# Group 2's statistics in the prologue, and three elements' attention weights transposed by TensorE, in a two-layer graph kernel

## The chip, the cores and the metric

The kernel runs on one core of a Trainium2 chip. The core has a matrix engine (TensorE, PE in the profile, its weight loads PEld), a vector engine (VectorE, DVE), a scalar engine (ScalarE, ACT), a general engine (GpSimd, POOL) and a queue that issues nearly all DMA transfers here (SyncE, SP). Each executes its own instructions in the order in which they were written; semaphores hold an instruction back until what it needs is there.

The metric is the time of the device for one execution, in microseconds (us). A profile of one execution shows when every instruction started and how long it took.

## The reference

`x` is 128 batch elements of 128 nodes with 512 features, `adj` one weighted 128x128 adjacency matrix with its diagonal. All is fp32.

```python
# layer 0: graph convolution
h = relu(layernorm(x));  norm_adj = adj * d[:, None] * d[None, :]      # d = deg ** -0.5
x = x + einsum('nm,bmo->bno', norm_adj, h @ W0) + b0
# layer 1: attention, 8 heads of 64, masked by adj
h = relu(layernorm(x))
q, k, v = h @ Wq + bq, h @ Wk + bk, h @ Wv + bv
attn = softmax(q k^T / 8 + (1 - adj) * -1e9)
x = x + (attn v) @ Wo + bo
```

## The kernel before

**Tiling.** The 128 elements go through in 32 groups of 4; an element's 128 nodes fill the 128 partitions. A projection (512x512 weights) of a group is computed by a scheme with seven block products instead of eight, in some cases at two levels (`Projection`). It needs sums of blocks of its left side, made by DVE or POOL: `Operands.combine` writes four sums at L362 to L365 and, for the second level, nine more by `combine_one` at L90. Weights get the same at the start: `combine_w` (L264, four sums) and `combine_inner` (L90, nine). The prepared weights are stored to DRAM (`keep_w`, L191) and reloaded for each later group (`reload_w`, L992).

**Rounds.** The main loop runs over rounds t, of blocks W, Q, K, V and Y. Round t computes the graph convolution's projection of group t+1 (W), queries, keys and values of group t (Q, K, V), and the output projection of group t-1 (Y). Each block has seven steps, W0 to W6 and so on. Round 0 has no W and no product in Y. A prologue goes before it: it prepares constants and brings groups 0 and 1 through the first layer, the second with the seven products of `gcn_weight(1)`, between which other work is placed.

**The order of the work.** Nothing reorders at run time. A table `plan` names for each round and place what else is to be issued there: `at(t, "Q3", f, ...)` appends a call to the place Q3 of round t. The function `block` walks through the places, issues the table's calls of step n (place `Q3`), then the product and its first reads (`step(3)`), then the calls of `Q3b`, then further reads (`rest(3)`). One place's calls are in the order of their appending, and those of the prologue are appended last. So each engine's order follows from this walk, SP's too.

**What belongs to one element:** `ln1` and `ln2` compute statistics for half a group: per element one DVE instruction at L314 and one at L315, then `scale`: DVE L319 (`ve`), POOL L320 (`rs`) and two of POOL L322 (`nb`). `gcn_norm` and `norm_h` (ACT L333) apply them and give `h`. `gcn_mix` (PE L605, tile `pa`) multiplies `h` by the adjacency; ACT copies it into the operand tile (L610). `transpose_h` turns `h` of layer 1 by PE (L674, tile `pt`), with a copy by ACT (L675). `gcn_operands` and `attention_operands` call `combine`; in groups 0 and 1 the latter's first four sums run on DVE, in later groups on POOL.

**Attention.** `scores` (PE L750) goes to four PSUM banks; DVE reads it with the mask (L757), or ACT without it (L754) and POOL adds it later (`add_mask`, L765). Then `row_max` (DVE L769), `exponentials` (ACT L777) and `softmax_end` (DVE L784, POOL L785). `attend` needs the weights transposed. In groups 0 to 30 this goes through DRAM: `split_att` has ACT separate the halves of each number (L790) and stores them (`planes`, L791), and `turn_att` reads them back by a DMA transpose on SP (L794), into the buffer of element b-1. In group 31, `transpose_att` does it in place: PE turns eight heads (L801, tile `paT`, through two PSUM buffers that `pa`, `pt`, `pss` and `po` share) and ACT makes two copies (L803). The four calls of `attend` (PE L816, ACT L823) of group t-1 stand at V0 of round t, elements 2 and 3 first; after them come the scores of group t, whose element 1 uses the banks that `attend` of elements 0 and 1 filled.

**Shared buffers around the change.** The tile `op_o` is the operand tile of attention, but before that it holds the weights v (in round 0) and then o (in round 1) while they are prepared: `combine_inner v`, `keep_w v`, `load_w o`, `combine_w o`, `combine_inner o` and `keep_w o` follow each other on it, and then ACT writes the first `attend` result to it.

Of the kernel before, what the change touches and what calls it, by code (L numbers as in the profile page):

```python
# [93 lines left out]
def kernel(  # L94
# [640 lines left out]
    def att_of(g, b):  # L735


        return att_buf[(b - g) % (GB + 1)]

    def scores(g, b):  # L740
        cols = slice(b * P, (b + 1) * P)
        if b == 3:
            pair = [small_bank(f"pss_{g}_{b}_{p}") for p in range(2)]
        else:
            pair = [bank[k] for k in (("b", f"a{1 - turn[0]}") if b == 1 else ("d0", "d1"))]
        pss = [t.rearrange("q (c k) -> q c k", c=NC) for t in pair]
        for c in range(NC):
            for p in range(2):
                rows = slice(p * HD, (p + 1) * HD)
                nc.tensor.matmul(pss[p][:, c, :], qs[g][rows, c, cols], ks[g][rows, c, cols], start=True, stop=True)  # L750
        for p in range(2):
            dst = att_of(g, b)[:, p * NC : (p + 1) * NC, :]
            if masked_apart(g, b):
                nc.scalar.activation(dst, pss[p], AF.Copy, scale=SCALE)  # L754
            else:
                mask = msk.unsqueeze(1).to_broadcast([P, NC, P])
                nc.vector.scalar_tensor_tensor(dst, pss[p], SCALE, mask, ALU.mult, ALU.add)  # L757
# [47 lines left out]
    def attend(g, b):  # L805
        if g not in op_o:
            op_o[g] = op_norm if g == NG - 1 else op_att
        aT = att_of(g, b if g == NG - 1 else b - 1)
        if b == 2 or b == 3:
            po = small_bank(f"po_{g}_{b}")  # L810
        else:
            po = bank["b" if b == 0 else f"a{1 - turn[0]}"]
        for c in range(NC):
            for p in range(2):
                h = 2 * c + p
                nc.tensor.matmul(  # L816
                    po[p * HD : (p + 1) * HD, c * P : (c + 1) * P],
                    vs[g][:, b, h * HD : (h + 1) * HD],
                    aT[:, p * NC + c, :],
                    start=True,  # L820
                    stop=True,
                )
        nc.scalar.copy(op_o[g].blocks_of(b), po.rearrange("p (c n) -> p c n", c=NC))  # L823
# [20 lines left out]
    for t in range(-1, NG + 1):  # L844
# [3 lines left out]
        if 0 <= t - 1 < NG - 1:  # L848
            g = t - 1

            for first, final, place, f, *args in (
                ("W1", "-Y6", "Q0", turn_att, 0),
                ("W4b", "-Y6b", "W1b", split_att, 1),
                ("W5", "-Y3", "W2", exponentials, 2, 0, H // 2),
                ("W6", "-Y4", "W3", exponentials, 2, H // 2, H),
                ("Q0b", "-Y5b", "W4b", softmax_end, 2),
                ("Q1", "-Y5", "W5", exponentials, 3, 0, H // 2),
                ("Q2", "-Y6", "W6", exponentials, 3, H // 2, H),
                ("Q0", "Q1", "Q2", turn_att, 1),
                ("Q2b", "Q0b", "Q0b", softmax_end, 3),  # L860
                ("Q4b", "Q0b", "Q3b", split_att, 2),
                ("Q6b", "Q2", "Q5b", split_att, 3),
                ("K1", "Q2", "K0", turn_att, 2),
                ("K3", "Q5", "K2", turn_att, 3),
            ):
                place = first if t == 1 else final if last else place
                at(t - place.startswith("-"), place.strip("-"), f, g, *args)
            for b in (2, 3, 0, 1):
                at(t, "V0", attend, g, b)
        if t == 0:  # L870

            at(0, "Q0b", ln2, 1, 0)
            at(0, "Q1b", ln2, 1, 1)
            at(0, "K6", norm_h, 1, 0)
            at(0, "K6", norm_h, 1, 1)
            at(1, "W0", transpose_h, 1, 0)
            at(1, "W0", norm_h, 1, 2)
            at(1, "W1", transpose_h, 1, 1)
            at(1, "W1", norm_h, 1, 3)
            at(1, "W2", transpose_h, 1, 2)  # L880
            at(1, "W3", transpose_h, 1, 3)
            at(1, "W3", attention_operands, 1)
            at(2, "W6", attention_residual, 1, 0)
            at(2, "W6", attention_residual, 1, 1)
        elif 1 <= t + 1 < NG and t >= 0:
            g = t + 1
            at(t, "K0b" if g < NG - 1 else "Q0b", ln2, g, 0)
            at(t, "K3b" if g < NG - 1 else "Q3b", ln2, g, 1)
            if g == NG - 1:

                places = ("Q3", "Q4", "Q5", "Q5", "Q6", "Q6", "K1", "K2", "K2")
                steps = ((norm_h, 0), (norm_h, 1), (transpose_h, 0), (norm_h, 2), (transpose_h, 1), (norm_h, 3))
                steps += ((transpose_h, 2), (transpose_h, 3))
            else:
                places = ("V1", "V2", "V2b", "V3", "V5", "V6", "Y1", "Y2", "Y5")
                steps = ((norm_h, 0), (norm_h, 1), (split_h, 0), (split_h, 1), (norm_h, 2), (norm_h, 3))
                steps += ((transpose_h, 2), (transpose_h, 3))
                at(t, "Y0", turn_h, g)
            for place, (f, b) in zip(places, steps):
                at(t, place, f, g, b)  # L900
            at(t, places[8], attention_operands, g)
            at(t + 1, "Q3", attention_residual, g, 0)
            at(t + 1, "Q4", attention_residual, g, 1)
# [5 lines left out]
            at(t, "W5" if t > 1 else "W0", load_x, t + 2, (1,))  # L909
        if 2 <= t + 2 < NG:  # L910
            g = t + 2
            at(t, "Q0b", ln1, g, 0, (0,), ())
            at(t, "Q1b", ln1, g, 0, (1,), (0, 1))
            at(t, "Q3b", ln1, g, 1)
            places = (("Q3", "Q5"), ("Q4", "Q6"), ("Q5b", "K1"), ("Q6", "K2"))
            for b, (norm, mix) in enumerate(places):
                at(t, norm, gcn_norm, g, b)
                at(t, mix, gcn_mix, g, b)
            at(t, "K2" if t > 0 else "V1b", gcn_operands, g)
            at(t, "Y1" if t > 0 else "K3", gcn_residual, g, 0)  # L920
            at(t, "Y2" if t > 0 else "K3", gcn_residual, g, 1)
        if 0 <= t < NG:
# [16 lines left out]
            else:  # L939
# [5 lines left out]
                else:  # L945
# [1 line left out]
                    at(t, "V5b", exponentials, g, 1, 0, H // 2)  # L947
                    at(t, "V6", exponentials, g, 1, H // 2, H)
                    at(t + 1, "W1b", softmax_end, g, 1)
                at(t, "Y3b", split_att, g, 0)  # L950
                at(t, "V6b", row_max, g, 2)
                at(*((t, "Y1") if t > 0 else (1, "W0")), add_mask, g, 3)
                at(*((t, "Y3b" if g == NG - 2 else "Y6b") if t > 0 else (1, "W4b")), row_max, g, 3)
# [67 lines left out]
    def prologue():  # L1021
# [35 lines left out]
        for n, product in enumerate(gcn_weight(1)):  # L1057
# [3 lines left out]
            elif n == 2:  # L1061
                transpose_h(0, 0)
                norm_h(0, 2)
            elif n == 3:
                transpose_h(0, 1)
                norm_h(0, 3)
                combine_w("q", nc.gpsimd)
            elif n == 4:
                transpose_h(0, 2)
            elif n == 5:  # L1070
                transpose_h(0, 3)
                attention_operands(0)
# [91 lines left out]
```

## Time and profile before

| What | us |
|---|---|
| median of 3 runs (lowest, highest) | 2301.77 (2300.41, 2305.13) |
| the profiled execution | 2300.24 |
| its span, first to last instruction | 2298.4 |
| PE busy | 2274.9 (99%) |
| DVE busy | 1863.2 (81%) |
| POOL busy | 1862.8 (81%) |
| ACT busy | 1366.8 (59%) |
| bytes moved by DMA | 566.46 MB, 246 GB/s |

The profiled execution's own time is 1.84 us above its span. Times in a profile count from the start of the span. A row of a timeline gives start, length, engine, line, operation, output and inputs, shapes and count; brackets at the end give the idle time before it and what ended it. Rows merge neighbours of one kind, and matmuls overlap, so a row's length holds the last one's tail. A row of the waits gives the engine, tile and line that waited and what for, the total, how often, and the longest.

### The profile page before, as it was taken

How to read it: one execution, taken by the hardware profiler on the slowest of the kernel's cores; microseconds unless marked ns; L12 is line 12 of the kernel's file. 1: busy time of each engine (PE TensorE's matmuls, PEld its weight loads, DVE VectorE, ACT ScalarE, POOL GpSimd, SP SyncE). 2: the span in 40 equal slices, each digit the busy share in tenths (PEclk: the TensorE clock that was granted, in tenths of full speed). 3: DMA queues.
4: the chain of work that ended last, by engine and by line, in shares of the span. 5: the costliest groups of instructions: out<-in, count | busy, mean ns of one | idle time of the engine just before them, and what ended most of it. 6: DMA issues, size and time to landing. Idle time of an engine off the chain costs nothing.

```text
span 2298.4 us, 50576 instructions
## 1 busy us (share of the span) xinstructions
PE 2274.9 (99%) x18127; PEld 2131.8 (93%) x18127; DVE 1863.2 (81%) x4832; ACT 1366.8 (59%) x3553; POOL 1862.8 (81%) x1927
## 2 busy tenths in 40 slices
PE   8999999999999999999999999999999999999999
PEld 8889999999999999999999999999999999999998
DVE  6778888788888888887888888888877888888876
ACT  3555666655656556566566565566665665655654
POOL 6898888788888787888888887879877788878864
PEclk9999999999999999999999999999999999999999
DMA  6388978889887888788897788987888988789873
GB/s 200 123 260 272 270 247 257 238 251 298 240 253 235 252 269 257 257 244 246 249 304 244 242 240 248 278 258 253 241 248 248 285 251 244 241 249 289 235 230 115
DMA packets 455259, 566.46 MB, mean 246 GB/s; under 512 B 332640, under 2 KB 339936, under 8 KB 454496
## 3 DMA queue, kind: packets, MB, share of 16 engines
q1 hardware_dynamic: 455008, 563.23, 81.2%
q8 instruction: 144, 2.36, 0.4%
q14 instruction: 107, 0.88, 0.1%
HBM read 358.68 MB, written 124.26 MB: 210 GB/s over the span
## 4 chain that ended last, share of the span: by engine, by line
PE 74%; POOL 6%; DMA 6%; DVE 3%; issue 2%; ACT 2%; SPq 0%; POOLq 0%; DVEq 0%; ACTq 0%
PE bank_a L388 27%; PE bank_d L388 16%; PE bank_c L388 8%; PE bank_b L388 8%; PE pa L605 4%; DMA xt<-in_x_dram 4%; PE bank_d L750 3%; PE po L816 3%; POOL xt L337 2%; DVE xt L429 2%; PE pss L750 1%; PE bank_b L816 1%; PE bank_a L816 1%; PE bank_b L750 1%; POOL att L765 1%
## 5 line engine op out<-in xcount | busy, mean ns | idle before, releaser
L777 ACT ACTIVATE att<-att,nmx 128x128 f32<-128x128 f32 x1024 | 396.3, 391 | 0.9 <-DVE nmx L769 0.9
L388 PE MATMUL bank_a<-op_h,w 128*128 128x256 f32 x1488 | 353.3, 380 | 0.0
L785 POOL TENSOR_TENSOR att<-att,rsm 128x1024 f32<-128x1024 f32 x128 | 243.1, 1900 | 80.3 <-DVE rsm L784 79.9
L388 PEld LDWEIGHTS bank_a<-op_h,w 128*128 128x128 f32 x1488 | 270.0, 191 | 29.4
L429 DVE TENSOR_TENSOR xt<-xt,bank_d 128x512 f32<-128x512 f32 x732 | 268.8, 415 | 19.2 <-DVE xt L429 1.4
L790 ACT COPY att<-att 128x2048 uint16<-128x2048 uint16 x124 | 234.9, 1895 | 60.5 <-POOL att L785 60.5
L333 ACT ACTIVATE h<-xt,nb,rs 128x512 f32<-128x512 f32 x254 | 207.3, 817 | 69.2 <-POOL nb L322 67.4
L711 ACT ACTIVATE q<-bank_a,bqk 128x256 f32<-128x256 f32 x192 | 80.6, 471 | 265.4 <-PE bank_a L388 265.4
L320 POOL TENSOR_TENSOR rs<-ve,mhalf 128x2 f32<-128x2 f32 (+1 forms) x129 | 91.3, 708 | 180.1 <-DVE ve L319 179.7
L90 POOL TENSOR_TENSOR op_o<-op_o 128x256 f32<-128x256 f32 x297 | 210.1, 734 | 10.0
L388 PE MATMUL bank_d<-op_h,w 128*128 128x128 f32 (+1 forms) x1712 | 216.9, 278 | 0.7 <-issue 0.3
L90 POOL TENSOR_TENSOR op_a<-op_a 128x256 f32<-128x256 f32 x279 | 197.1, 730 | 14.9 <-DVE op_a L365 5.3
L388 PEld LDWEIGHTS bank_d<-op_h,w 128*128 128x128 f32 x1712 | 203.1, 192 | 5.0 <-issue 3.4
L90 POOL TENSOR_TENSOR op_h<-op_h 128x256 f32<-128x256 f32 x270 | 190.7, 731 | 13.1 <-DVE op_h L365 3.8
L777 ACT ACTIVATION_READ_ACCUMULATOR att<-att,nmx 128x1 f32 x1024 | 194.8, 190 | 0.0
L314 DVE BATCH_NORM_STATS2 st<-xt 128x6 f32<-128x512 f32 x256 | 172.9, 675 | 20.3 <-DMA xt<-in_x_dram 20.0
L388 PE MATMUL bank_a<-w,op_o 128*128 128x256 f32 x768 | 181.7, 379 | 0.0
L388 PE MATMUL bank_a<-w,op_h 128*128 128x256 f32 x744 | 179.1, 384 | 0.0
L388 PE MATMUL bank_a<-w,op_a 128*128 128x256 f32 x744 | 176.9, 381 | 0.2 <-DVE xt L439 0.2
L439 DVE TENSOR_TENSOR xt<-bank_a,xt 128x512 f32<-128x512 f32 x252 | 166.9, 684 | 11.5 <-PE bank_a L388 3.9
L757 DVE SCALAR_TENSOR_TENSOR att<-bank_d,msk 128x512 f32<-128x512 f32 x128 | 82.4, 686 | 104.7 <-PE bank_d L750 96.2
L769 DVE TENSOR_REDUCE nmx<-att 128x8 f32<-128x1024 f32 x128 | 154.9, 1210 | 0.0
(188 smaller groups left out, 5936.2 us busy)
## 6 DMA issues: line engine op xcount, KB each, us to landing
w<-wd_v SPq DMA_DIRECT2D x93, 704.0 KB, 5.6
w<-wd_o SPq DMA_DIRECT2D x93, 704.0 KB, 7.1
planes<-att SPq DMA_DIRECT2D x124, 512.0 KB, 4.5
w<-wd_q SPq DMA_DIRECT2D x90, 704.0 KB, 6.1
w<-wd SPq DMA_DIRECT2D x87, 704.0 KB, 5.6
xt<-in_x_dram SPq DMA_DIRECT2D x63, 512.0 KB, 6.5
out_dram<-xt SPq DMA_DIRECT2D x62, 512.0 KB, 4.1
planes_h<-att SPq DMA_DIRECT2D x29, 512.0 KB, 3.0
```

Of the source, the lines that this page charges most:

```text
L90: engine.tensor_tensor(twice(out), twice(x), twice(y), ALU.subtract if minus else ALU.add)
L314: nc.vector.bn_stats(self.st[:, j, :], self.src[:, j, :])
L333: nc.scalar.activation(h, src[:, j, :], AF.Relu, bias=nb[:, j : j + 1], scale=rs[:, j : j + 1])
L388: nc.tensor.matmul(out, lhsT, rhs, start=start, stop=True, skip_group_check=True)
L429: nc.vector.tensor_tensor(dst, dst, src, f)
L439: nc.vector.tensor_tensor(t, src.rearrange("p (r f) -> p r f", r=2), t, ALU.add)
L750: nc.tensor.matmul(pss[p][:, c, :], qs[g][rows, c, cols], ks[g][rows, c, cols], start=True, stop=True)
L769: nc.vector.tensor_reduce(nmx, att_of(g, b), AX.X, ALU.max, negate=True)
L777: nc.scalar.activation(att[:, h, :], att[:, h, :], AF.Exp, bias=nmx[:, h : h + 1], scale=1.0, accum_out=sm[:, h : h + 1])
L785: nc.gpsimd.tensor_tensor(att, att, rsm.unsqueeze(2).to_broadcast([P, H, P]), ALU.mult)
L790: nc.scalar.copy(planes, halves)
L816: nc.tensor.matmul(po[p * HD : (p + 1) * HD, c * P : (c + 1) * P], vs[g][:, b, h * HD : (h + 1) * HD], aT[:, p * NC + c, :], start=True, s ...
```

## The change

Statistics of group 2 (`ln1(2, 0)` and `ln1(2, 1)`) are issued between the products of `gcn_weight(1)` in the prologue instead of in steps Q0 to Q3 of round 0. Elements 2 and 3 of group 0 and element 3 of group 30 no longer go through `split_att` and `turn_att`; `transpose_att` turns them in place, at K3 and K5 of round 1 and at K1 of round 31, and `attend` reads them where they are. `split_att(0, 0)` moves from Y3b of round 0 to W1 of round 1, `attention_operands(1)` from W3 to W4b of round 1, and the two halves of `attention_residual(1)` from W6 to Q5 and K1 of round 2.

```diff
+    def turned_in_place(g, b):
+        return g == NG - 1 or (g, b) in ((0, 2), (0, 3), (NG - 2, 3))
...
     def attend(g, b):
...
-        aT = att_of(g, b if g == NG - 1 else b - 1)
+        aT = att_of(g, b if turned_in_place(g, b) else b - 1)
...
                 place = first if t == 1 else final if last else place
+                if f in (split_att, turn_att) and turned_in_place(g, args[0]):
+                    continue
                 at(t - place.startswith("-"), place.strip("-"), f, g, *args)
+            if t == 1:
+                at(1, "K3", transpose_att, g, 2)
+                at(1, "K5", transpose_att, g, 3)
+            elif last:
+                at(t, "K1", transpose_att, g, 3)
...
             at(1, "W3", transpose_h, 1, 3)
-            at(1, "W3", attention_operands, 1)
-            at(2, "W6", attention_residual, 1, 0)
-            at(2, "W6", attention_residual, 1, 1)
+            at(1, "W4b", attention_operands, 1)
+            at(2, "Q5", attention_residual, 1, 0)
+            at(2, "K1", attention_residual, 1, 1)
...
-            at(t, "Q0b", ln1, g, 0, (0,), ())
-            at(t, "Q1b", ln1, g, 0, (1,), (0, 1))
-            at(t, "Q3b", ln1, g, 1)
+            if t > 0:
+                at(t, "Q0b", ln1, g, 0, (0,), ())
+                at(t, "Q1b", ln1, g, 0, (1,), (0, 1))
+                at(t, "Q3b", ln1, g, 1)
...
-                at(t, "Y3b", split_att, g, 0)
+                at(*((t, "Y3b") if t > 0 else (1, "W1")), split_att, g, 0)
...
             elif n == 3:
                 transpose_h(0, 1)
                 norm_h(0, 3)
+                ln1(2, 0)
                 combine_w("q", nc.gpsimd)
             elif n == 4:
                 transpose_h(0, 2)
+                ln1(2, 1)
```

## The prediction

> **What bounds the kernel now.** The page first: the span is 2298.4 us and TensorE (PE) is busy for 2274.9 us of it.
>
> ```profile
> span 2298.4 us, 50576 instructions
> PE 2274.9 (99%) x18127; PEld 2131.8 (93%) x18127; DVE 1863.2 (81%) x4832; ACT 1366.8 (59%) x3553; POOL 1862.8 (81%) x1927
> ```
>
> No other engine is near its limit over the whole span. So a gain must be idle PE, and an added PE instruction costs its own time. PE's waits come next.
>
> ```profile
> PE bank_c L388 <- DVE xt L429: 5.1, 12, 1.3
> PE pa L605 <- ACT h L333: 4.1, 1, 4.1
> PE bank_b L750 <- ACT op_o L823: 3.7, 1, 3.7
> PE pt L674 <- ACT h L333: 2.1, 1, 2.1
> ```
>
> The three long waits occur once each. PE's timeline puts them at 53.72-57.81 (round 0), 99.95-102.07 and 147.02-150.76 (both round 1). From round 2 the first matmul of `attend` returns every 70.07 us (16 of 29 rounds: up to 0.9 more).
>
> A wait costs more than its length. Two windows after two of them, and then PE's rows after the first:
>
> ```profile
> 58.48:61.89 3.41, 3.41 (x12) 2.87 (x11) 1.31 (x3) 1.29 (x3) 3.11 (x6) 0.50 0.00 0
> 150.64:154.05 3.41, 3.29 (x28) 3.29 (x30) 1.05 (x2) 0.56 (x2) 3.31 (x4) 0.50 0.87 288
> ...
> 57.81 1.52 PE L605 MATMUL pa<-ant,h 128*128 128x128 f32 x8 [4.09 <-ACT h L333]
> 59.12 3.25 PE L388 MATMUL bank_a<-op_h,w 128*128 128x256 f32 x8
> 62.21 1.05 PE L605 MATMUL pa<-ant,h 128*128 128x128 f32 x8
> 63.10 1.89 PE L388 MATMUL bank_c<-op_h,w 128*128 128x256 f32 x8
> ```
>
> A window lists its stretch, its length and the busy time of PE, weight loads, DVE, ACT and POOL; the third figure from the end is the granted clock: 0.50 for 3.41 us, and equally in 102.85-106.27. The same sixteen matmuls took 4.40 us (57.81 to 62.21) and would take 0.89 + 1.73 = 2.62 at full clock.
>
> **What the skill says.** "TensorE: Matmul & The Clock Gate", Part 1: a free-running window of 3413 ns decides the clock, and an idle one brings half rate. The trace agrees on the length and the half; the idle it needs is here less than a window: the slices before the slow ones held 2.74, 2.12 and 3.42 us of idle, while one with 1.30 (113.09-116.50) had no slow slice after it. Part 4, PE-mode transpose: a transpose does not count as busy for that clock (no run here shows it; 0.87 us at a time stays below the 1.30 that did no harm), and it goes to PSUM and needs a copy after it; so it is in the last round: eight `paT` transposes in 0.87 us (start to next start), two copies of 0.59. "GPSIMD Engine Reference", Specifications: POOL shares its SBUF interfaces with DVE and contends with two-input DVE instructions. Agrees: DVE's L362-L365 take 1.26 and 1.10 us while POOL runs at 42-47, 0.69 where POOL is idle (106-109).
>
> **The change, part by part.**
>
> *Statistics of group 2 in the prologue.* At 53.72 PE wants `gcn_mix(2,0)`; its `h` waits for POOL's nb, and that for DVE's statistics, queued behind those of `ln2(1)`. Moved, they come after DVE's row at 36.90; x of group 2 landed by 24 (DMA is idle from then). Two times 1.90 us go into DVE gaps of 1.47, and the copies for `attention_operands(0)` are ready at 42.26: DVE is about 0.2 late, on nobody's path. Gain: 4.09 + 1.78 = 5.87.
> POOL is the risk. It runs in order, and nb(2,0) now stands ahead of `combine_w q`:
>
> ```profile
> 35.74 5.19 POOL L264 TENSOR_TENSOR w<-w 128x512 f32<-128x512 f32 x4
> 40.89 8.26 POOL L90 TENSOR_TENSOR w<-w 128x256 f32<-128x256 f32 x9
> ```
>
> Ready at 35.74, POOL waits for ve(2,0): 37.50 + 1.90 = 39.40, then 1.26 for rs and nb: `combine_w q` starts at 40.7. Its last operation makes T1, which PE wants at 46.65. At 1.30 each: 45.9, no wait. But from 42.5 to 47 it contends with DVE's L362-L365; the nine L90 there now run at some 1.15 us against 0.73, a factor 1.57, and so T1 comes at 47.6. I take 1.0 lost (bounds 0 and 2.0; at 2.0 perhaps 1.7 of slow clock too). nb(2,1) and the later POOL work have slack. Net 4.87; round 1 starts at 95.62 - 4.87 = 90.75.
>
> *Round 1, W.* Times here are counted from the block's first PE transpose, 95.62 before and 90.75 in the forecast. `split_att(0,0)` (1.90 us) leaves the place ahead of h(1,2), so the transposes lose their wait: ACT ends its exponentials 2.87 after the block starts, h(1,2) at 4.17, and PE wants it at 4.20. That is 2.12 + 1.72 of slow clock. But the split now precedes the copies of pt 2 and 3, the second of which ends at 8.1, and `attention_operands(1)` comes after DVE's bank_a and bank_b reads. DVE before:
>
> ```profile
> 106.12 0.68 DVE L362 TENSOR_TENSOR op_h<-op_h 128x512 f32<-128x512 f32 x1
> ...
> 108.90 0.68 DVE L439 TENSOR_TENSOR xt<-bank_a,xt 128x512 f32<-128x512 f32 x1
> 110.01 1.21 DVE L769 TENSOR_REDUCE nmx<-att 128x8 f32<-128x1024 f32 x1
> 111.14 2.26 DVE L429 TENSOR_TENSOR xt<-xt,bank_d 128x512 f32<-128x512 f32 x6
> 113.32 1.28 DVE L439 TENSOR_TENSOR xt<-bank_a,xt 128x512 f32<-128x512 f32 x2
> 114.85 0.87 DVE L429 TENSOR_TENSOR xt<-xt,bank_c 128x256 f32<-128x256 f32 x2
> ```
>
> PE's next bank_c phase waits for that last row (the 1.30 at 115.77, 20.15 into the block). In the new order PE ends the bank_a product at 7.9, DVE reads it until 8.6 and bank_b until 9.05, so L362 starts at 9.05 (before: 10.5, set by ACT's last copy). From there to the end of the bank_c row DVE has no gap: L362-L365 2.8, row maximum 1.15, bank_d 2.2, bank_a 1.2, bank_b 0.35, bank_c 0.8, together 8.5 (before 9.6, with the two reads inside that are now ahead, 1.1), plus 0.15 of contention with POOL's softmax multiply: 17.7. PE, no longer late, wants it at 14.33: a wait of 3.4 replaces 1.30. Gain of the block 20.15 - 17.7 = 2.45; 3.4 exceeds the 2.12 that halved the clock, so -1.7: net 0.75. Unknown: whether two windows share the idle so that neither trips (0 instead of 1.7).
>
> *Round 1, attention weights 2 and 3 by PE.* Removed: two ACT splits (3.8 us), two stores to DRAM and two DMA transposes. Added: sixteen PE transposes at 0.109, 1.74 us; four ACT copies of 0.59, where ACT loses more than that; a 0.32 wait at 139.40 is covered. Net -1.42. The multiplies of elements 2 and 3 end (about 111 and 115) long before the transposes (some 130), and the two PSUM buffers have been copied by then. What it frees is SP. At `attend`, ACT waits 8.63, put down to POOL, but its first copy starts at 149.14 as `keep_w o`, which reads the same tile, lands (SP's own list: 7.8 us on wd_o). That store was issued at 139.82 behind DMA transposes issued at 134.92-139.73, though its data was complete at 135.04. Now: the v store leaves at 98.6 (POOL, 4.9 earlier), lands 10.35 later; `load_w o` is issued by 110.9 and landed at 114.9; POOL combines from 115.5 (element 3's multiply first) for 5.2 + 1.3 + 6.5: 128.5; the store lands 8.9 later, 137.4. `attend` starts at 142.21 - 7.3 + 1.7 + 1.4 = 138.0, and the scores want their bank 4.75 later, 1.9 after ACT's first copy: anything up to 141 is free. Gain 3.74 + 1.89 (150.76 to 155.43 took 4.67; the same rows take 2.78 at 2192.88) = 5.63.
> SP, moved past: planes(0,0) now stands behind `load_w o` (110.9 instead of 100.84). Landing 4.5, turn 4.4, planes(0,1) and a reload 0.9, wait 2.4, turn 2.6: SP is free by 126, and turn(0,1) lands by 133; `attend` wants it after 140. x of group 3 is issued sooner; The reloads of v and o weights, next in SP's queue, have over 10 us to spare.
>
> *Group 30.* Eight transposes, 0.87 lost. Before, `attend` did not wait there (2243.72), and the 0.39 wait at 2226.86 belongs to the split of element 2, which stays.
>
> *`attention_residual(1)`* goes from W6 to Q5 and K1 of round 2: two POOL adds of 2.36 into POOL gaps of 2.91 and 2.12. Nothing.
>
> **Sum:** 4.87 + 0.75 - 1.42 + 5.63 - 0.87 = 8.96. On the profiled execution (2300.24, span plus 1.84) 2291.3; it lies 1.53 below the median 2301.77, so 2292.8.
>
> **Rivals.**
> 1. *DVE does not hold PE in W*, or no slow clock follows: gain 10.7 to 13 and 2289 to 2291. It decides if L362 can start by about 7.5. For: DVE has gaps before it. Against: it needs pt 3's copy (8.1), and its rows after that leave no gap.
> 2. *POOL becomes the bound in round 0*: T1 is 2 us late and halves the clock; gain 6.3, 2295.5. For: contention; against: 45.9 without it.
> 3. *The wait at `attend` stays* (the v store or POOL is late): gain 3.3, 2298.5, no change. Against: its data was ready at 135.04 already.
> 4. *Slower:* SP is held by turn(0,0) and turn(0,1), now later, and `keep_w o` waits behind them. Landing after 141 costs one for one, plus 1.7; the whole gain is gone at 148, and 2306.5 (slower by 0.2%) needs 153, SP free only at 144 instead of 126. The longest hold by one turn in this trace is 8.50 us (2223.95); two of them give 138, so a late landing of planes must be added.
>
> **From these, the numbers.** Chances: forecast 0.50, rival 1 0.18, rival 2 0.12, rival 3 0.11, rival 4 0.09. A measurement here can tell some 0.2% (4.6 us) from no change. Faster 0.79, same 0.12, slower 0.09. The long rounds can turn short or back by 0.8 each, a few us: range 2288 to 2299; it takes in rivals 1 to 3.
>
> **What would show it.** No PE wait at round 0's `gcn_mix`; one of 0-2 us before round 0's second q product; POOL's `combine_w q` near 41; no wait at pt 2; PE bank_c waiting some 3.4 us on DVE early in round 1's Q, then a half-clock slice; wd_o issued near 128; no wait at bank_b of the scores; `paT` rows in rounds 1 and 31. Wrong if bank_b still waits, or PE waits at `attend` for a DMA.

## The result, and the profile after

| | before | after |
|---|---|---|
| median of five runs (lowest, highest), us | 2301.77 (2298.88, 2305.13) | 2291.74 (2291.30, 2293.39) |
| the profiled execution | 2300.24 | 2293.39 |
| its span | 2298.4 | 2291.6 |

The ratio is 0.9958, with an interval of 0.9943 to 0.9972: some 10 us faster, where 9 were forecast (2292.8 against 2291.74). Measured again later, beside other kernels, it was 2291.28 against 2300.06, a ratio of 0.9957 [0.9944, 0.9969]. Lines of the program from L740 on have other numbers in the kernel after: `scores` is at L754, the softmax multiply at L789, `split_att` at L794 and L795, `turn_att` at L798, `transpose_att` at L805 and L807, `attend` at L820 and L827, `reload_w` at L1004 (a few lines off in some experiments). The page of the kernel after, in the lines that answer to those shown of before:

```profile
span 2291.6 us, 50617 instructions
PE 2273.9 (99%) x18151; PEld 2132.9 (93%) x18151; DVE 1868.3 (82%) x4832; ACT 1364.3 (60%) x3556; POOL 1860.9 (81%) x1927
```

PE has 24 more matmul rows, the transposes, and is busy 1.0 us less. Its waits:

```profile
PE bank_c L388 <- DVE xt L429: 7.4, 8, 3.8
PE bank_d L754 <- DVE k L439: 2.2, 1, 2.2
```

The waits at `pa` (4.1), `pt` (2.1) and bank_b of the scores (3.7) are gone, all three as forecast. The 3.8 at bank_c was forecast (3.4). The second line was not forecast: it is new. PE's timeline shows where both lie, and how far ahead of before PE is:

```profile
53.50 1.05 PE L605 MATMUL pa<-ant,h 128*128 128x128 f32 x8
...
75.02 2.08 PE L754 MATMUL bank_d<-k,q 64*128 64x128 f32 x16 [2.24 <-DVE k L439]
...
93.51 0.60 PE L674 MATMUL pt<-ident,h 128*128 128x128 f32 x4
...
111.68 0.71 PE L388 MATMUL bank_c<-w,op_a 128*128 128x128 f32 x4 [3.76 <-DVE xt L429]
...
140.89 1.97 PE L820 MATMUL po<-att,v 128*64 128x128 f32 x32
148.31 1.99 PE L388 MATMUL bank_a<-w,op_h 128*128 128x256 f32 x8
```

Both waits are followed by a slice at half clock, like the three that the prediction named of before: 112.65 to 116.07 after the wait at bank_c, and after the new one this window (the granted clock is the third figure from the end):

```profile
75.10:78.50 3.40, 3.40 (x32) 3.40 (x34) 3.40 (x5) 0.00 (x0) 3.32 (x5) 0.51 0.24 87
```

Set beside before, and beside what the terms of the forecast add up to at each mark:

| PE starts | before | after | ahead | forecast |
|---|---|---|---|---|
| the first scores of round 0 | 78.80 | 75.02 | 3.78 | 4.87 |
| the first `pt` of round 1 | 95.62 | 93.51 | 2.11 | 4.87 |
| `po` of round 1 | 142.21 | 140.89 | 1.32 | 4.20 |
| the first V product of round 1 | 155.43 | 148.31 | 7.12 | 9.83 |

(0.20 of each lead is older than the change: PE's last `pa` row of the prologue starts at 23.76 in before and at 23.56 after, where the two programs are still the same.) So the total came out near the forecast, but the path to it did not. 2.76 us were lost in round 0; the rest went about as said.

**The new wait.** The timelines of DVE and of POOL in round 0's K, after:

```profile
65.98 0.69 DVE L439 TENSOR_TENSOR k<-bank_b,k 128x512 f32<-128x512 f32 x1 [3.74 <-PE bank_b L388]
66.59 2.74 DVE L264 TENSOR_TENSOR op_o<-op_o 128x512 f32<-128x512 f32 x1
69.25 2.84 DVE L292 SCALAR_TENSOR_TENSOR att<-wo,bv_c,att 128x512 f32<-128x512 f32 x1
...
66.43 5.10 POOL L337 TENSOR_TENSOR xt<-xt,b 128x1024 f32<-128x1024 f32 x2
```

The same in before:

```profile
67.56 2.58 DVE L290 TENSOR_SCALAR att<-wo,bv_c 128x512 f32<-128x512 f32 x1
72.07 0.69 DVE L439 TENSOR_TENSOR k<-bank_b,k 128x512 f32<-128x512 f32 x1 [1.93 <-PE bank_b L388]
...
73.50 1.21 DVE L292 SCALAR_TENSOR_TENSOR att<-wo,bv_c,att 128x512 f32<-128x512 f32 x1
...
67.05 5.29 POOL L337 TENSOR_TENSOR xt<-xt,b 128x1024 f32<-128x1024 f32 x2
```

POOL adds group 2's bias (`gcn_residual`, L337) at the same time in both kernels, 66.43 and 67.05. PE and DVE come to K six us earlier than before. In before the adds fell on L290, which took 2.58 us, and then DVE had 1.93 us to spare; after, they fall on L264 and L292, which stand ahead of the reads of k. These two took 2.74 and 2.84 instead of 0.91 and 1.21: 3.46 us. PE waited for 2.24 of them, so it had about 1.2 to spare.

**The end of round 1.** SP's own list of what it issued, after:

```profile
127.72 1.01 SPq L1004 DMA_DIRECT2D w<-wd_v  x2
132.56 0.32 SPq L191 DMA_DIRECT2D wd_o<-op_o  x1
...
141.66 1.99 SPq L1004 DMA_DIRECT2D w<-wd_o  x4
```

`wd_o` was stored at 139.82 in before, behind two DMA transposes:

```profile
134.92 4.81 SPq L794 DMA_TRANSPOSE att<-planes  x2
139.82 0.53 SPq L191 DMA_DIRECT2D wd_o<-op_o  x1
```

After, its reload at 141.66 waits for the landing, so the store took 9.0 us (issued at 132.56, landed at 141.59); ACT copies the first `po` at 142.08 as PE has it, and the scores wait for nothing.

### The profile page after: what moved, and what is told of

Its sections match the earlier page's. It is cut to its first block, busy times and chain, and to the rows that moved or that the text cites. A ratio compares the mean times of both kernels' runs of the same rounds, so it can differ in the third digit from the quotient of the medians.

```text
span 2291.6 us, 50617 instructions
## 1 busy us (share of the span) xinstructions
PE 2273.9 (99%) x18151; PEld 2132.9 (93%) x18151; DVE 1868.3 (82%) x4832; ACT 1364.3 (60%) x3556; POOL 1860.9 (81%) x1927
## 4 chain that ended last, share of the span: by engine, by line
PE 88%; POOL 3%; DMA 3%; DVE 3%; issue 1%; ACT 1%; SPq 0%; POOLq 0%; DVEq 0%; ACTq 0%
PE bank_a L388 31%; PE bank_d L388 19%; PE bank_c L388 10%; PE bank_b L388 10%; PE pa L605 5%; PE bank_d L754 3%; PE po L820 3%; DMA xt<-in_x_dram 2%; PE pss L754 1%; PE bank_b L820 1%; PE bank_a L820 1%; PE bank_b L754 1%; PE pt L674 1%; POOL xt L337 1%; DVE xt L429 1%
## 5 line engine op out<-in xcount | busy, mean ns | idle before, releaser
L789 POOL TENSOR_TENSOR att<-att,rsm 128x1024 f32<-128x1024 f32 x128 | 242.7, 1897 | 82.3 <-DVE rsm L788 82.3
L794 ACT COPY att<-att 128x2048 uint16<-128x2048 uint16 x121 | 229.3, 1895 | 66.0 <-POOL att L789 66.0
L314 DVE BATCH_NORM_STATS2 st<-xt 128x6 f32<-128x512 f32 x256 | 173.0, 676 | 18.4 <-DMA xt<-in_x_dram 18.3
L439 DVE TENSOR_TENSOR xt<-bank_a,xt 128x512 f32<-128x512 f32 x252 | 167.2, 684 | 10.2 <-PE bank_a L388 2.7
```

The lines of the kernel that those rows point to most:

```text
L314: nc.vector.bn_stats(self.st[:, j, :], self.src[:, j, :])
L439: nc.vector.tensor_tensor(t, src.rearrange("p (r f) -> p r f", r=2), t, ALU.add)
L789: nc.gpsimd.tensor_tensor(att, att, rsm.unsqueeze(2).to_broadcast([P, H, P]), ALU.mult)
L794: nc.scalar.copy(planes, halves)
```

## The experiments

All kernels but the last are edits of the changed one; "V" is the start of round 1's first V product, the mark at which a kernel's gain in the first two rounds can be read (before 155.43, after 148.31). Two things lie on V that are no part of an edit: PE's last `pa` row of the prologue, up to which all the programs are alike, starts between 22.48 and 24.52 from one profile to the next, and a half-clock slice more or less is some 1.7 us. The table after the attempts takes the first away and counts the second.

The kernels were measured in four groups, each with before beside it on the same chip, and each ratio is to that: 2300.77 for the four kernels with one part undone, 2299.64 for the next four (up to the three together), 2300.06 for the multiply behind L365, the row maximum and the kernel after again, 2299.14 for the last attempt. So a median set against the 2291.74 of the kernel after can be off by 1 or 2 us.

### One part of the change undone

**Group 30's element 3 by DMA again**

```diff
-        return g == NG - 1 or (g, b) in ((0, 2), (0, 3), (NG - 2, 3))
+        return g == NG - 1 or (g, b) in ((0, 2), (0, 3))
...
-            elif last:
-                at(t, "K1", transpose_att, g, 3)
```

> Only group 30's element 3 goes back to split and DMA transpose. Theory: its eight TensorE transposes buy nothing. The first V product of round 1 stays at 148.3 us; round 31 loses the 0.87 us of the transposes; about 0.9 us faster than the changed kernel (2290.8). Rival: the DMA transpose would now be late, PE waits at attend of round 31 and the time is the same or longer.

2290.52 (2289.83 to 2292.09), ratio to before 0.9955 [0.9938, 0.9971]; V 148.26. 1.2 us below the kernel after, where 0.87 was forecast, but the difference is no larger than the spread of the runs. In the kernel after, the eight transposes of round 31 took 0.87 (2225.72 to 2226.59), and the wait of 0.39 stayed (2219.51). From that wait to the end of the span, the four kernels that turn this element by DMA need 71.44 to 71.46 us, the kernel after 72.10 and 72.09. So this part costs 0.65 us and returns nothing: the profiles say so, the times alone could not.

**Group 0's elements 2 and 3 by DMA again**

```diff
-        return g == NG - 1 or (g, b) in ((0, 2), (0, 3), (NG - 2, 3))
+        return g == NG - 1 or (g, b) in ((NG - 2, 3),)
...
-            if t == 1:
-                at(1, "K3", transpose_att, g, 2)
-                at(1, "K5", transpose_att, g, 3)
-            elif last:
+            if last:
                 at(t, "K1", transpose_att, g, 3)
```

> Only elements 2 and 3 of group 0 go back to split and DMA transpose. Theory: SP's DMA transposes hold up the store of the prepared o weights, ACT waits for it at attend. Round 1 starts at 93.5 as in the changed kernel; the store is issued behind the transposes at 136 to 139 instead of 132.6; PE waits 3 to 4 us at the scores' bank_b, then a half-clock slice; 16 transposes (1.4 us net) are saved; the first V product at about 152.4 instead of 148.3, some 4 us slower than the changed kernel. Rival (the wait's named releaser, POOL's sums of op_a, is the cause): no wait more than in the changed kernel, first V product at 146.9, 1.4 us faster.

2300.66 (2298.95 to 2308.14), ratio 1.0003 [0.9993, 1.0012]: the whole gain is gone, more than the 4 us expected. V 156.12. PE's waits, and then SP's list:

```profile
PE bank_b L754 <- ACT op_o L827: 3.1, 1, 3.1
PE po L820 <- DMA att<-planes: 2.5, 2, 1.7
```

```profile
135.96 4.21 SPq L798 DMA_TRANSPOSE att<-planes  x2
140.25 0.53 SPq L191 DMA_DIRECT2D wd_o<-op_o  x1
```

The store stands behind two DMA transposes again and leaves at 140.25, and ACT's copies wait for its landing until 149.51 (12.28 of idle), as in before; in addition PE, now earlier, waits at `attend` for the transposes themselves. The rival, that POOL's other work and not the store holds ACT's copies, is refuted.

**Group 2's statistics in round 0 again**

```diff
-            if t > 0:
-                at(t, "Q0b", ln1, g, 0, (0,), ())
+            at(t, "Q0b", ln1, g, 0, (0,), ())
...
-                ln1(2, 0)
...
-                ln1(2, 1)
```

> Only the statistics of group 2 go back to round 0. Theory: the 4.1 us wait at the first gcn_mix of round 0 and a half-clock slice return (5.9), while the 2.2 us wait at the first scores and its slow slice (4.1) go, since PE is late there again: round 1 starts at 95.6 instead of 93.5, about 2 us slower. Rival (the wait at the scores has nothing to do with the statistics coming early): it stays, and round 1 starts at 99.4, 5.9 us slower.

2293.47 (2292.44 to 2293.63), ratio 0.9962 [0.9949, 0.9975]. The wait at `pa` (4.1) is back, now with two half-clock slices, the wait at the scores is gone, round 1 starts at 96.05 and V at 150.77. Against this profile the statistics in the prologue are worth 2.5 us of PE's time at V, and 1.7 by the medians; against the second profile of the kernel after, which has as many half-clock slices, 0.9 at V. It is half of what the prediction gave them at most.

**Round 1's W in the order of before**

```diff
-                at(*((t, "Y3b") if t > 0 else (1, "W1")), split_att, g, 0)
+                at(t, "Y3b", split_att, g, 0)
...
-            at(1, "W4b", attention_operands, 1)
+            at(1, "W3", attention_operands, 1)
```

> Only the order in W of round 1 goes back: split of element (0,0) at Y3b of round 0 and the attention operands of group 1 at W3. Theory (DVE bounds this block whichever order): the 2.1 us wait at pt 2 and a half-clock slice return, the bank_c wait falls from 3.8 to 1.3 and loses its half-clock slice; bank_c's phase comes 20.2 after the block's start instead of 18.2; the first V product of round 1 within 0.5 us of 148.3, total the same. Rival (the order is worth the 4 us that it takes away): first V product at 152.3, 4 us slower.

2289.55 (2287.63 to 2294.54), ratio 0.9951 [0.9935, 0.9967]; V 146.69. PE waits 2.1 at `pt`, 1.2 at bank_a and 1.3 at bank_c in this block, and 2.2 at the scores as in the kernel after. The block's bank_c phase starts 19.52 after the block, against 18.17 in the new order: the order is worth 1.35 us. But the old order spreads its idle over three waits, and in this profile the clock was never halved between 40 and 165, not after the 2.2 at the scores either. That is worth more than the order. The theory held in that DVE sets the end of the block in both orders; the half-clock slice that it had after the wait at `pt` did not come, and V is 1.6 lower than in the kernel after, not within 0.5 (0.7 of it from the earlier start). The rival, that the order is worth 4 us, is refuted.

### The cause of the new wait

**The bias adds at K0 instead of K3 of round 0**

```diff
-            at(t, "Y1" if t > 0 else "K3", gcn_residual, g, 0)
-            at(t, "Y2" if t > 0 else "K3", gcn_residual, g, 1)
+            at(t, "Y1" if t > 0 else "K0", gcn_residual, g, 0)
+            at(t, "Y2" if t > 0 else "K0", gcn_residual, g, 1)
```

> One move on top of the changed kernel: POOL's two adds of the first layer's bias to group 2 (2.4 us each) from K3 of round 0 to K0, ahead of the q weights' second-level sums. Theory: at K3 they run beside DVE's two-input instructions and stretch these from 1.2 to 2.7 us, so DVE reads k's bank_d late. Then L264 and L292 of K3 and K4 take at most 1.3 us each, the wait at the first scores (2.24) and its half-clock slice vanish, and round 1 starts at 89.5 to 90.5 instead of 93.5: 3 to 4 us faster. Rival (DVE has too many instructions there, whatever POOL does): the wait stays within 1 us of 2.24 and round 1 starts at 92.5 or later.

2289.42 (2287.88 to 2290.07), ratio 0.9956 [0.9942, 0.9971]; V 146.34. The wait at the scores is gone and round 1 starts at 89.75, inside the 89.5 to 90.5 expected. L264 and L292 in K take 0.68 and 1.22. Its timelines of DVE and of POOL show the adds on two other instructions, which nobody waits for, and a second place of the same kind in round 1:

```profile
59.77 5.02 DVE L264 TENSOR_TENSOR op_o<-op_o 128x512 f32<-128x512 f32 x2
...
99.75 2.27 DVE L363 TENSOR_TENSOR op_h<-op_h 128x512 f32<-128x512 f32 x1
...
59.12 5.11 POOL L337 TENSOR_TENSOR xt<-xt,b 128x1024 f32<-128x1024 f32 x2
...
99.13 2.34 POOL L789 TENSOR_TENSOR att<-att,rsm 128x1024 f32<-128x1024 f32 x1
```

PE and DVE are 3.8 us earlier in round 1, POOL about 2; so POOL's softmax multiply (L789) now lies on DVE's L363, which takes 2.27 us, and PE's bank_c waits 4.96 instead of 3.76, with two half-clock slices instead of one. Of the 3.76 us gained by the start of round 1, 1.97 are left at V.

**The bias adds of round 0 left out**

```diff
-            at(t, "Y1" if t > 0 else "K3", gcn_residual, g, 0)
+            if t > 0:
+                at(t, "Y1", gcn_residual, g, 0)
```

(and the same for the second half).

> Leaves out the first layer's bias add for group 2 (two POOL adds in K3 of round 0), nothing else. Theory (these adds stretch DVE): no DVE instruction at L264 or L292 above 1.3 us after K2, no wait at the first scores, round 1 starts at 89.5 or earlier. Rival (DVE is full by itself): the wait stays above 1.2 us.

2284.12 in one run of a kernel that leaves work out; no wait at the scores, round 1 at 89.34, V at 144.12, 4.2 earlier. DVE's timeline:

```profile
66.40 1.12 DVE L264 TENSOR_TENSOR op_o<-op_o 128x512 f32<-128x512 f32 x1
67.44 1.21 DVE L292 SCALAR_TENSOR_TENSOR att<-wo,bv_c,att 128x512 f32<-128x512 f32 x1
```

Nothing but POOL's two adds was taken away, and the two instructions take 1.12 and 1.21. That shows the cause of the new wait.

### Attempts at something faster

**A new order of W: fewer rows ahead of bank_c on DVE**

```diff
-            at(1, "W4b", attention_operands, 1)
+            at(1, "W3", attention_operands, 1)
-                at(*((t, "Y3b") if t > 0 else (1, "W1")), split_att, g, 0)
+                at(*((t, "Y3b") if t > 0 else (1, "W3")), split_att, g, 0)
```

(`turn_att(0, 0)` goes to W3 with it, and `row_max(0, 3)` from W4b to Q0b.)

> On top of the changed kernel: split of (0,0) to W3 behind the last transpose of h (its DMA transpose with it), the attention operands of group 1 to W3, and the row maximum of (0,3) from W4b to Q0b. Theory (DVE's chain up to bank_c sets the block): operands start 7.7 instead of 9.0 after the block's start and the chain is 1.15 shorter; PE waits about 1.6 for the read of bank_a and under 1 at bank_c, no half-clock slice; bank_c's phase at 16.2 instead of 18.2, first V product of round 1 at 144.6 instead of 148.3, 3.7 us faster. Rival (ACT's copies or POOL's second-level sums set it): bank_c or the q product after it waits as long as before, first V product no earlier than 147.5.

2290.66 (2287.49 to 2291.84), ratio 0.9962 [0.9950, 0.9973]; V 147.86. A miss: not 3.7 faster. The bank_c wait is gone, but PE waits 3.02 at bank_a (106.08), because L363 lies on POOL's softmax multiply here too and takes 2.27. The order only chose another bank to wait at.

**This, the bias adds at K0 and group 30 by DMA together**

```diff
-            at(t, "Y1" if t > 0 else "K3", gcn_residual, g, 0)
+            at(t, "Y1" if t > 0 else "K0", gcn_residual, g, 0)
...
-        return g == NG - 1 or (g, b) in ((0, 2), (0, 3), (NG - 2, 3))
+        return g == NG - 1 or (g, b) in ((0, 2), (0, 3))
...
-            elif last:
-                at(t, "K1", transpose_att, g, 3)
```

(on top of the new order of W; the second half of the adds likewise).

> Group 30 by DMA, the bias adds at K0 and the new order in W together, on top of the changed kernel. If each does what its theory says and they add up: 0.9 + 3.5 + 3.7 = 8.1 us faster than the changed kernel, 2283.6. Rival (they share a bound: POOL's preparation of the o weights and its store are not moved forward, and attend waits for them): the scores' bank_b waits 1 to 4 us, and 2286 to 2289 results.

2288.73 (2285.97 to 2290.11), ratio 0.9953 [0.9939, 0.9966]; V 145.44. The lowest median of a kernel that leaves nothing out, and still 3 us from the kernel after, not 8. Round 1 starts at 88.57, five us earlier (1.1 of it from the start), and PE then waits 3.75 at bank_a, at 102.16: this time L365 is the one that takes 2.27. The time lies where the rival put it, but its wait at the scores' bank_b did not come either; what the parts share is POOL's multiply on DVE's sums.

**Element 1's softmax multiply behind L365** (on top of the bias adds at K0)

```diff
-                    at(t + 1, "W1b", softmax_end, g, 1)
+                    at(t + 1, "W5b", softmax_end, g, 1)
-                ("W4b", "-Y6b", "W1b", split_att, 1),
+                ("Q2b", "-Y6b", "W1b", split_att, 1),
-                ("Q0", "Q1", "Q2", turn_att, 1),
+                ("Q4", "Q1", "Q2", turn_att, 1),
```

> On the kernel with group 2's residual adds at K0, element 1's softmax multiply of group 0 moves from W1b to W5b of round 1 (its split to Q2b, its turn to Q4), so that POOL no longer runs it beside DVE's L362 to L365. Theory (that multiply stretched L363 from 0.69 to 2.27 us and so made PE's bank_c wait 4.96): L363 takes at most 1.1, round 1 still starts at 89.7, the bank_c wait is 3.2 to 3.6, round 1's first V product starts at 144.7 (146.34 without the move), and the time is 1.6 below that kernel's 2289.4, so about 2287.8. Rival (PE's bank_c wait is set by ACT's or PE's own work, and DVE only happens to be last): L363 is short, the wait stays above 4.5, and the first V product stays at 146.3. A second rival: the later split and turn of element 1 are late at attend, and PE waits there for a DMA by 1 us or more.

2293.65 (2292.04 to 2294.28), ratio 0.9969 [0.9956, 0.9981]: 2.4 us slower than the kernel after beside it (2291.28), though the two sets of runs touch (2292.04 against 2292.78). The theory was right on its own place. L363 takes 0.69 and the wait at bank_c is 3.51. But V is at 151.76. PE waits 4.24 at bank_b of the scores for ACT's copies of `attend`, as in before. SP's list:

```profile
119.73 0.37 SPq L795 DMA_DIRECT2D planes<-att  x1
129.10 1.75 SPq L798 DMA_TRANSPOSE att<-planes  x1
...
131.57 0.38 SPq L191 DMA_DIRECT2D wd_o<-op_o  x1
...
145.19 1.96 SPq L1004 DMA_DIRECT2D w<-wd_o  x4
```

The planes of element 1 now stand behind two reloads (118.64) and land late. SP stands at the turn until 129.10, the third reload (130.91) goes just ahead of the store, and the store takes 13.6 us to land instead of 9.0. Nobody waits for the turn itself; ACT's copies wait for the store, and PE for them: it is the wait that the change had removed. This is close to the prediction's fourth rival (SP held by a turn, the store behind it), brought about by a move of one multiply.

**The row maximum at Q0b too, and group 30 by DMA** (on top of the one before)

```diff
-                at(*((t, "Y3b" if g == NG - 2 else "Y6b") if t > 0 else (1, "W4b")), row_max, g, 3)
+                at(*((t, "Y3b" if g == NG - 2 else "Y6b") if t > 0 else (1, "Q0b")), row_max, g, 3)
...
-        return g == NG - 1 or (g, b) in ((0, 2), (0, 3), (NG - 2, 3))
+        return g == NG - 1 or (g, b) in ((0, 2), (0, 3))
...
-            elif last:
-                at(t, "K1", transpose_att, g, 3)
```

> The same, with element 3's row maximum of group 0 also moved from W4b to Q0b (1.2 us of DVE out of the way of the bank_c row) and group 30's element 3 transposed by DMA again. Theory (DVE's chain sets the bank_c row): the bank_c wait is 2.0 to 2.5, the first V product starts at 143.5 (1.7 earlier still if no half-clock slice follows the shorter wait), the group 30 part gives 0.9, and the time is 2285.5. Rival: as where the row maximum was moved together with the transposes' order, the wait only goes to another bank (bank_a, 3 us or more) and the first V product stays at 144.5 or later; 2287.

2292.49 (2290.49 to 2294.66), ratio 0.9965 [0.9951, 0.9978]. The bank_c wait is 2.39, as the theory said, and the wait at the scores is 4.34, with two half-clock slices, so V is at 151.18 and not 143.5.

**Planes before reloads, and the weights o before element 3's multiply** (on top of the last one)

```diff
-                ("Q2b", "-Y6b", "W1b", split_att, 1),
+                ("Q0b", "-Y6b", "W1b", split_att, 1),
-                ("Q4", "Q1", "Q2", turn_att, 1),
+                ("Q1", "Q1", "Q2", turn_att, 1),
-                ("Q2b", "Q0b", "Q0b", softmax_end, 3),
+                ("Q5b", "Q0b", "Q0b", softmax_end, 3),
```

> The kernel with the residual adds at K0, the multiply of element 1 after L365 and the row maximum at Q0b, but with element 1's split at Q0b and its turn at Q1 of round 1 (so that its planes are stored before the second reload of wd_v), and element 3's softmax multiply after POOL's combine_inner o (Q2b to Q5b), so that the weights o are complete earlier. Theory (the 4.3 us wait at the scores came from the late landing of wd_o, whose store was issued at 130.4 right behind a late DMA transpose and took 13.3 us): element 1's turn is issued by 125, wd_o is issued near 127 and lands by 137, no wait at bank_b of the scores, the bank_c wait stays at 2.4, round 1's first V product starts at 143.5 (145.2 with one half-clock slice), and the time is 2286.5. Rival (the store takes its 13 us in any case, since reloads and the x loads share the DMA engines in that stretch): the wait at the scores stays at 1.5 or more, and the time is 2289 or above.

2291.29 (2287.62 to 2292.01), ratio 0.9964 [0.9951, 0.9978]; V 147.76. The rival was right on the store. SP's list:

```profile
127.06 1.01 SPq L1002 DMA_DIRECT2D w<-wd_v  x2
128.16 0.38 SPq L191 DMA_DIRECT2D wd_o<-op_o  x1
...
142.05 2.96 SPq L1002 DMA_DIRECT2D w<-wd_o  x4
```

The store leaves 4.4 us earlier than in the kernel after and lands 0.4 later; two reloads left just ahead of it. PE doesn't wait at the scores only because it was held up elsewhere. ACT's split now starts at 109.78, 5.58 of idle behind the late multiply; the copy of q stands behind it (113.14), DVE waits 4.21 for that, and PE 3.13 for DVE, at 115.67.

**The kernel after, again**

> The changed kernel itself beside these, on the same chip, for a comparison free of differences between chips: 2291.7, as measured first, within 1.5; a first V product of round 1 at 148.3 in its profile. If it comes out below 2290, the gains read against its first figure are in doubt by that much.

2291.28 (2286.76 to 2292.78): as first measured. But its V is at 149.84, 1.5 later than in its first profile, with the same waits of 2.2 and 3.75. The difference is one more slice of 3.41 us at half clock: two in a row at the wait at bank_c (110.97 to 117.80; the wait ends at 112.19), not one.

**All of them side by side.** The second column is V less the start of PE's last `pa` row of the prologue; the third counts the half-clock slices from 40 us to V.

| kernel | V less start | slices | median below before, same chip |
|---|---|---|---|
| before | 131.67 | 3 | |
| after | 124.75 | 2 | 10.03 |
| after, again | 126.75 | 3 | 8.78 |
| group 30 by DMA | 123.74 | 1 | 10.25 |
| group 0's two elements by DMA | 132.72 | 3 | 0.11 |
| statistics in round 0 | 127.71 | 3 | 7.30 |
| W as before | 123.85 | 0 | 11.22 |
| adds at K0 | 122.56 | 2 | 10.22 |
| adds left out | 120.74 | 1 | one run |
| new order of W | 123.94 | 1 | 8.98 |
| the three together | 122.96 | 2 | 10.91 |
| multiply behind L365 | 128.05 | 3 | 6.41 |
| row maximum too | 127.93 | 3 | 7.57 |
| planes first, weights o first | 124.95 | 2 | 7.85 |

None of these beats the kernel after by more than its runs differ. The three best medians (2288.73, 2289.42, 2289.55) lie 2 to 3 us below its first one, but 10.2 to 11.2 below before on their own chips, where the kernel after has 10.0 and 8.8. Between rows with equal slices, the adds at K0 save 2.2 us up to V, and the new order of W adds nothing to that. Later, the profiles drift apart again: from V to round 31's wait of 0.39 they take between 2065.8 and 2071.4 us (before 2071.4, the kernel after 2071.2 and 2068.2), and what decides that no run here shows.

## Why the prediction was right, and where it was not

**The sum.** 8.96 was forecast. The two profiled executions differ by 6.85, the medians by 10.03 and, measured again, 8.78. The marks account for it: 7.12 at V and 0.23 from there to round 31's wait of 0.39, less 0.53 after that wait. The other 3.2 us between 6.85 and 10.03 are the place of the two profiled executions among their runs: that of before is 1.53 below its median, that of after 1.65 above. The second profile of the kernel after has one halved slice more, some 1.7 us, and 3.0 us less in the long rounds, for the same code. So the agreement to 1 us is partly luck. What carries the result is that the terms removed are seen removed.

**Statistics in the prologue: forecast 4.87, measured 2.11.** Up to the scores the gain was higher than forecast: without the new wait the scores would have started at 72.78, 6.02 ahead. The term that was mis-sized first is T1: 1.0 us for POOL's contention, measured 0.12 (POOL was done with T1 at 46.44, PE's second q product started at 46.49, 0.33 after the matmul before it, where 0.21 to 0.22 is the step). POOL did start `combine_w q` at 40.47, as forecast. The prediction took its factor 1.57 from POOL's additions of 128x256 (of the nine in its row, four take 1.17 or 1.18 instead of 0.73) and let it lengthen what was left of the four of 128x512 from 42.5 on. These took 1.27, 1.27, 1.60 and 1.71: a meeting added 0.33 to 0.44 us to one of them, as it does to one half as long, and not its own half. DVE's L363 and L364 took 1.64 and 1.65, which cost nobody anything. The step that failed is the one after it, "nb(2,1) and the later POOL work have slack". The work of POOL had slack, and nobody waited for it. But where it lies in time decides which of DVE's instructions it stretches, and PE's gain moved DVE's K under POOL's adds: 2.24 of wait and 1.67 of slow clock, 3.91 in all. Leaving the adds out gave 4.17 at the start of round 1, moving them 3.76 (4.0 both, when the start of the prologue's last `pa` row is taken off).

The sign of this was in the profile of before: L290 took 2.58 us there and 0.94 after, and the Trainium skill says why. The prediction went by "GPSIMD Engine Reference", Specifications, that the two engines contend; "SBUF — State Buffer", Who interferes with whom, is more exact: a DVE instruction with two SBUF inputs (or in one of its two-port modes) and a POOL instruction that reads SBUF exclude each other for a whole instruction, and the loser is blocked. The runs agree. In the fourteen profiles, 163 rows of DVE's two-input instructions (L264, L292, L362 to L365) take more than 1.0 us, and every one ends 0.54 or 0.55 us after the end of a POOL instruction (after: L292 at 72.09 against 71.54, L362 at 103.83 against 103.28; adds at K0: 64.79 against 64.24 and 102.02 against 101.47). L290 ends 0.28 after (70.14 against 69.85 in before). So DVE pays what is left of POOL's instruction, up to 2.35 us for an add of 128x1024, and POOL's next one starts beside DVE's and pays some 0.45 (2.80 instead of 2.35, 1.17 instead of 0.73). It is not one factor for both sides, as the prediction had it.

**W: forecast 0.75, measured about 0.4.** bank_c came 18.17 after the start of the block (17.7 forecast; L362 met the softmax multiply and took 1.32, where 0.15 of contention had been allowed) with 3.76 of wait (3.4) and a half-clock slice after it. The block gained 1.98 (20.15 less 18.17), where 2.45 was forecast, and the slice took 1.6 of it, matmul by matmul against before. With the transposes' 1.42 against it, PE should have lost 0.67 from the first `pt` to `po`; it lost 0.79, because the transposes cost about 1.2 net.

**Transposes by PE and `attend`.** The rows of `paT` at 131.80 and 137.31 take 0.87 each, and the gain from `po` to V is 5.80, where 5.63 was forecast. `wd_o` left at 132.56 and not 128.5: round 1 started 2.76 later, and POOL's multiply of element 3 went ahead of the weights o and ended at 119.7 (115.5 forecast with element 3 in it). Up to 141 was free by the prediction, and the landing came at 141.6 with PE 2.9 later than forecast too; so it decided nothing, with 0.5 us to ACT's first copy and about 2 more to the scores' bank. The runs with the multiply moved showed how thin that is. Undoing this part alone took back all the gain: by its waits, the statistics and the order of W only brought PE sooner to `attend` and to the store.

**Group 30: forecast 0.87 lost, measured 0.53 against before and 0.65 against the runs without it.** It returned nothing, as forecast.

**The rivals.** DVE does hold PE in W (rival 1 wrong), T1 was not late (2), the wait at `attend` did not stay (3), and the store was not held (4); rival 4's mechanism is real, as the two kernels with the later turn show. What was missing among the rivals was one in which the gain itself moves two engines onto each other.

## What to carry to other kernels

When a change brings one engine forward in time, compare what now runs side by side, not only who waits for whom: POOL and DVE can stretch each other's instructions with no semaphore between them. Price such a meeting, for DVE, by what is left of POOL's instruction when DVE's begins, and look in the profile for rows that are long in one place and short in another; a long row in an idle stretch today is a wait tomorrow. In a dense schedule, a freed wait is worth what the next tie on each queue leaves of it: the attempts above mostly removed the wait they were aimed at and lost the gain to the one behind it.

## What was not expected of the hardware

- **POOL stretches DVE's two-input instructions past its own end, and most others not at all.** With both inputs in SBUF, a `tensor_tensor` of 128x512 takes 0.67 to 0.69 us where POOL runs nothing, 1.1 to 1.65 beside POOL's shorter instructions, and 2.27 to 2.84 beside adds and multiplies of 128x1024; all the stretched rows end 0.54 or 0.55 us after one of POOL's. L290, with one tensor input, was stretched too (2.58 in before) and ended 0.28 after, and L319 on 128x2 took up to 1.29 instead of 0.17, so two inputs are not needed. Most other forms were not: in the profile before, 315 rows of L439 (one input from PSUM), 149 of L314 (statistics) and 124 of the row maximum L769 began while one of POOL's adds or multiplies ran, and the longest took 0.69, 0.70 and 1.22.
- **Where a wait lies on the clock's grid decides what it costs.** In each profile the half-clock slices start on one grid of 3.413 us. Cut along it from 40 us on, the thirteen profiles that have such a slice there say: a window at full clock in which PE idled (the window less PE's busy time) for 1.99 us or more was followed by a slow one (22 of 22), one with 1.91 or less was not, but for a single case (1.69); a slow window in which PE idled for 0.74 or more was followed by another slow one (6 of 6), with 0.44 or less by full clock (23 of 23). So waits of one length at bank_c cost nothing, one slice or two:

| kernel | wait at bank_c | idle in the two windows that it lies on | slices |
|---|---|---|---|
| group 30 by DMA | 3.73 | 1.91 and 1.83 | 0 |
| after | 3.76 | 1.25 and 2.51 | 1 |
| after, again | 3.75 | 2.53 and 1.22, the second one slow | 2 |

The first row is the case that the prediction called unknown. The fixed grid is the free-running window of the Trainium skill's "TensorE: Matmul & The Clock Gate", Part 1, but the page speaks of a whole window of 3413 ns idle, and 1.99 was enough here. The grid lies elsewhere in each execution, so the same kernel has 2 or 3 slices; from 40 to 165 us the profiles hold 0 to 3, some 1.7 us each, enough to hide every difference between the last kernels.

- **A store's landing depends on what was queued just ahead.** `wd_o` took 8.4 to 9.2 us to land where the reload of `wd_v` ahead of it had left 4 us or more before (ten profiles, before among them), 10.0 where it had left 3.0 before (group 30 by DMA), and 13.3 to 13.8 where it had left within 1.2 us (the last three attempts). The runs show the times, and not how the two share the DMA engines.
